# The experts' stage with TensorE in written order and the survey cut into parts

## The chip, the cores and the metric

The kernel runs on one core of a Trainium2 chip. Times are device microseconds (us) of one execution of the whole program. Five engines work side by side, each on its own queue of instructions: TensorE (PE, with its weight loads shown apart as PEld), VectorE (DVE), ScalarE (ACT), GpSimd (POOL) and SyncE (SP, which here only issues DMAs). An engine takes its instructions in order and each waits for what it needs from the others.

## The reference

Input x is 32 sequences of 256 tokens with 128 features, 8192 tokens in all, in f32. Two pre-norm layers follow each other. Each line below adds to x, and LN is a layer norm without weights.

```
x = x + causal_attention(LN(x))      # layer 0, 16 heads, queries and keys 128 wide per head
x = x + experts(LN(x))               # layer 0, 16 experts of width 64, and a shared one
x = x + hyperbolic_attention(LN(x))  # layer 1, 16 heads of 8
x = x + relu(LN(x) @ w1 + b1) @ w2 + b2
```

The experts are what this document is about:

```
scores = sigmoid(x @ gate_w.T);  choice = scores + e_bias
the best 2 of 4 groups of experts by the sum of their two best choices, then the best 4 experts in them
weight = scores of those 4 / their sum * 2.5
y = sum over the 4 of weight * (silu(x @ gate_e.T) * (x @ up_e.T)) @ down_e.T
y = y + (silu(x @ s_gate.T) * (x @ s_up.T)) @ s_down.T     # the shared expert
```

The kernel computes all 16 experts for every token and multiplies each hidden value by the token's weight for its expert, which is zero where the expert was not chosen.

## The kernel before

x stays in on-chip memory for the whole run, as 16 groups (`xg[g]`) of 512 tokens, four tiles of 128 tokens each. Four groups make a quad. The program goes through three stages.

1. `causal_attention`, up to about 1030 us. TensorE's order is written out by hand here (`tc.manual_schedule`), the other engines' order is the planner's.
2. `experts`, from about 1036 to 1520 us. This is the stage of the diff. It ends with a flag, read into a register, that picks the branch for layer 1.
3. `far_attention` with layer 1's feed-forward inside it, from about 1520 us. (The other branch, `hyperbolic_attention` and `feed_forward`, is in the program but not run on these inputs.) In it, `scores` (line 1118 on) makes two PSUM tiles, `sc0` and `sc1`, for the products of four heads.

The planner is the part of the compiler that orders instructions wherever no order is written by hand. It walks the program with estimated durations and, on each engine, takes what is ready, with what was written earlier first. So written order matters to it, but it also runs ahead. Which buffer an instruction may write is part of what it must wait for: a pool gives each tag a number of buffers, and a tile waits until its buffer's last readers are done.

**The experts' stage.** For each group g, `fetched(g)` brings the normed and transposed tokens `bxT` (line 671) and the weights `wb`, broadcast over partitions, in two DMAs of 1 MB (line 677), from DRAM, on SP's queue. It is called one group ahead, at chunk 1. Then come nine chunks: eight of two experts each (128 hidden rows) and the shared expert (64 hidden rows). A chunk is:

- `g_ps` (line 696) and `u_ps` (line 698) on PE, each one f32 product of 128x128 by 128x512, which the trace shows as two matmul passes
- Silu of `g_ps` into `act` on ACT (line 700)
- `act` times `u_ps` on DVE (line 701), then times `wb` on DVE (line 703; not for the shared expert)
- the down product of `act` into `y_ps` on PE (line 704), which adds up over the nine chunks

[...] After the nine chunks ACT copies the sum into `yT` (line 708), `add_transposed` turns it back with four PE transposes (line 109, in the PSUM tag `u`) and DVE adds it to `xg[g]` (line 110).

**The survey** of the group follows (`survey`, lines 605 to 642). It prepares layer 1 and collects the extremes that decide the branch: statistics on DVE (lines 612, 613), subtraction of the mean on POOL (line 614), four PE transposes into `xc_ps` (line 620, tag `w`), the copy `sxc` on ACT (line 622), its store to DRAM on SP (line 623), then for two halves the products for queries and keys (line 628, tag `w`, eight passes in all), their squares on ACT (line 633) and sums on DVE (line 634), and last five operations on DVE (lines 637 to 642).

**The preparation** of the last quad's routing runs inside the same loop, as 26 `pieces`: statistics of four groups, their deviations, for each group `normed` (POOL, line 504), `tokens` (PE transposes `rxT_ps`, line 511) and `scored` (`logits`, line 520), then `best_groups`, and for each group `weights` (DVE, five operations of 128x1024 and some small ones) and `turned` (PE transposes `wT_ps`, line 579). One piece is called after chunks 1, 3, 5 and 7, so four per group, until they are used up in group 6.

PE's order in this stage is the planner's. In the lines that are written, each chunk's down product follows its own `g_ps` and `u_ps`, and a group's transposes and survey come between its last chunk and the next group's first one.

Of the kernel before, what the change touches and what calls it, by code (L numbers as in the profile page):

```python
# [9 lines left out]
F32 = mybir.dt.float32  # L10
BF16 = mybir.dt.bfloat16
AF = mybir.ActivationFunctionType
ALU = mybir.AluOpType
AX = mybir.AxisListType
PSUM = bass.MemoryType.PSUM

P = 128
B, N, D = 32, 256, 128
T = B * N
TG = 4  # L20
GT = TG * P
NG = T // GT
QUAD = 4
EPS = 1e-5

H = 16
DH = D // H
# [4 lines left out]
NE, INTER = 16, 64  # L32
# [8 lines left out]
class Net:  # L41
# [562 lines left out]

    def survey(self, pool, psum, g):

        nc = self.nc
        mv = pool.tile([P, TG, 2], F32, tag="smv", name=f"smv{g}")
        xn = pool.tile([P, TG, D], F32, tag="sxn", bufs=1, name=f"sxn{g}")
        for t in range(TG):  # L610
            st = pool.tile([P, nc.vector.BN_STATS_DIM], F32, tag="sst", bufs=4, name=f"sst{g}_{t}")
            nc.vector.bn_stats(st, self.xg[g][:, t, :])
            nc.vector.bn_aggr(mv[:, t, :], st)  # L613
            nc.gpsimd.tensor_scalar(xn[:, t, :], self.xg[g][:, t, :], mv[:, t, 0:1], None, ALU.subtract)  # L614
        rv = self.rv[:, g]
        nc.vector.tensor_scalar(rv, mv[:, :, 1], EPS, None, ALU.add)
        nc.vector.reciprocal(rv, rv)
        ps = psum.tile([P, GT], F32, tag="w", name=f"xc_ps{g}")
        for t in range(TG):
            nc.tensor.transpose(ps[:, t * P : (t + 1) * P], xn[:, t, :], self.ident)  # L620
        xc = pool.tile([P, GT], F32, tag="sxc", name=f"sxc{g}")
        nc.scalar.copy(xc, ps)
        nc.sync.dma_start(out=self.xc[g], in_=xc)
        n2 = pool.tile([P, TG, 2 * H], F32, tag="sn2", name=f"sn2_{g}")
        for i in range(2):
            qk = psum.tile([P, 2, 2 * D], F32, tag="w", name=f"sqk{g}_{i}")
            for t in range(2):
                nc.tensor.matmul(
                    qk[:, t], xc[:, (2 * i + t) * P : (2 * i + t + 1) * P], self.w_qkv[:, 0 : 2 * D],
                    start=True, stop=True,  # L630
                )
            sq = pool.tile([P, 2, 2 * D], F32, tag="ssq", bufs=1, name=f"ssq{g}_{i}")
            nc.scalar.activation(sq, qk, AF.Square)
            nc.vector.tensor_reduce(
                n2[:, 2 * i : 2 * i + 2], sq.rearrange("p t (h d) -> p t h d", d=DH), AX.X, ALU.add
            )
        nc.vector.tensor_mul(n2, n2, rv.unsqueeze(2).to_broadcast([P, TG, 2 * H]))
        nc.vector.tensor_reduce(self.ends[:, 0, g : g + 1], n2, AX.XY, ALU.min)
        nc.vector.tensor_reduce(self.ends[:, 1, g : g + 1], n2, AX.XY, ALU.max)
        ra = self.ra[:, g].rearrange("p t s h -> p t (s h)")  # L640
        nc.vector.tensor_scalar(ra, n2, -1.0, 1.0, ALU.mult, ALU.add)
        nc.vector.reciprocal(ra, ra)

    def survey_result(self, pool, psum):

# [12 lines left out]
    def experts(self, prep):  # L658
        nc, tc = self.nc, self.tc
        NCH = NE * INTER // P  # L660
        w_g, w_u, w_d, s_g, s_u, s_d = (self.w_e[n] for n in ("w_g", "w_u", "w_d", "s_g", "s_u", "s_d"))
        with (
            tc.tile_pool(name="mo", bufs=2) as pool,
            tc.tile_pool(name="mops", bufs=2, space=PSUM) as psum,
        ):

            def fetched(g):


                xT = pool.tile([P, GT], F32, tag="xT", bufs=3, name=f"bxT{g}")  # L670
                nc.sync.dma_start(out=xT, in_=self.xt[g])
                wb = pool.tile([P, NCH, GT], F32, tag="wb", bufs=3, name=f"wb{g}")
                rows = self.rows[g].rearrange("(c e) t -> e c t", e=2)
                for c in range(0, NCH, 1 if g == 0 else NCH):
                    cs = slice(c, c + 1 if g == 0 else NCH)
                    for e in range(2):
                        nc.sync.dma_start(
                            out=wb[e * INTER : (e + 1) * INTER, cs], in_=rows[e, cs].partition_broadcast(INTER)
                        )
                return xT, wb  # L680

            pieces = self.preparation(NG // QUAD - 1, prep, psum, "w")
            ready = fetched(0)
            for g in range(NG):
                xT, wb = ready
                y_ps = psum.tile([P, GT], F32, tag="y", name=f"y_ps{g}")
                for c in range(NCH + 1):
                    if c == 1 and g + 1 < NG:
                        ready = fetched(g + 1)
                    shared = c == NCH  # L690
                    m = INTER if shared else P
                    wg = s_g if shared else w_g[:, c * P : (c + 1) * P]
                    wu = s_u if shared else w_u[:, c * P : (c + 1) * P]
                    wd = s_d if shared else w_d[:, c, :]
                    g_ps = psum.tile([P, GT], F32, tag="g", name=f"g_ps{g}_{c}")
                    nc.tensor.matmul(g_ps[:m, :], wg, xT, start=True, stop=True)  # L696
                    u_ps = psum.tile([P, GT], F32, tag="u", name=f"u_ps{g}_{c}")
                    nc.tensor.matmul(u_ps[:m, :], wu, xT, start=True, stop=True)  # L698
                    act = pool.tile([P, GT], F32, tag="act", bufs=3, name=f"act{g}_{c}")
                    nc.scalar.activation(act[:m, :], g_ps[:m, :], AF.Silu)  # L700
                    nc.vector.tensor_mul(act[:m, :], u_ps[:m, :], act[:m, :])  # L701
                    if not shared:
                        nc.vector.tensor_mul(act, act, wb[:, c])  # L703
                    nc.tensor.matmul(y_ps, wd, act[:m, :], start=c == 0, stop=shared)  # L704
                    if c % 2 == 1 and pieces:
                        pieces.pop(0)()
                yT = pool.tile([P, GT], F32, tag="yT", name=f"yT{g}")
                nc.scalar.copy(yT, y_ps)
                self.add_transposed(pool, psum, "u", g, yT)
                self.survey(pool, psum, g)  # L710
            self.survey_result(pool, psum)


# [793 lines left out]
```

## Time and profile before

| | us |
|---|---|
| median of the 3 runs | 2210.81 (2207.41 to 2212.19) |
| profiled execution, its own time | 2204.17 |
| span in the profile, first to last instruction | 2202.4 |
| experts' stage, first `g_ps` to the flag's last reduction | 1036.2 to 1518.1 |
| copies of `yT`, first and last of 16 | 1063.1 and 1503.5 |

Rows of the profile begin with the start and the length in us on the timeline, then engine, line, operation, the tiles written and read, their shapes and how many instructions were merged. What stands in square brackets is how long the engine had been idle before, and whose work ended that. In the list of waits the numbers are the total in us, the number of times and the longest. "PEclk" or "clock" is the share of its full clock that PE was granted. PE's busy time counts a matmul from its start to a modelled end, and successive matmuls overlap.

### The profile page before, as it was taken

Reading aid. Unit: us, or ns where it says so; the run is one execution under the profiler, and the core shown is the slowest. Engines: PE = TensorE matmul, PEld = TensorE weight load, DVE = VectorE, ACT = ScalarE, POOL = GpSimd, SP = SyncE. Lnnn points to the kernel's source line nnn. Section 1 sums busy time; section 2 is a strip of 40 time slices with the busy share of each in tenths; the row PEclk is TensorE's granted clock in tenths of the full one; section 3 lists DMA queues with packets and bytes.
Section 4 is the critical chain, followed back from the end, with each engine's and each line's share of the span. In section 5 each row is a group of like instructions: output and inputs, shape, how many; then the busy total and the mean of one; then the engine's idle time right before and its main releaser. Section 6 shows DMA issues by size and latency. Waiting matters only on the chain.

```text
span 2202.4 us, 38323 instructions
## 1 busy us (share of the span) xinstructions
PE 2063.9 (94%) x14083; PEld 1326.1 (60%) x14083; DVE 1517.5 (69%) x4804; ACT 1376.4 (62%) x2429; POOL 753.8 (34%) x841
## 2 busy tenths in 40 slices
PE   5999999999999999997999999996889999999997
PEld 4677777776777777774444433343556565665653
DVE  2666666569655875577558755554678888888885
ACT  1766677666776667663222222222888999999993
POOL 3000000100011000100111100001999999999994
PEclk8999999999999999998999999997899999999999
DMA  5000000000000000001743444400000000000000
GB/s 155 1 1 1 1 1 1 11 11 3 2 6 11 7 2 1 11 11 48 165 96 83 97 96 96 96 10 25 10 6 11 16 11 20 11 15 16 11 11 21
DMA packets 43940, 66.64 MB, mean 30 GB/s; under 512 B 3617, under 2 KB 16689, under 8 KB 43745
## 3 DMA queue, kind: packets, MB, share of 16 engines
q1 hardware_dynamic: 40960, 59.00, 11.2%
q0 software_dynamic: 1200, 3.78, 0.5%
q8 instruction: 114, 1.87, 0.3%
q10 hardware_dynamic: 1584, 1.34, 0.2%
q14 instruction: 82, 0.66, 0.1%
HBM read 50.99 MB, written 13.11 MB: 29 GB/s over the span
## 4 chain that ended last, share of the span: by engine, by line
PE 66%; DVE 14%; ACT 6%; POOL 6%; issue 6%; DMA 1%; POOLq 0%; ACTq 0%; SPq 0%; DVEq 0%
PE t_ps L258 10%; PE s L286 9%; PE y_ps L704 5%; PE fs L1123 5%; PE s L279 4%; PE g_ps L696 4%; DVE fv L1183 4%; PE av L335 4%; PE u_ps L698 3%; PE fav L1135 3%; POOL fv L1193 3%; PE pa_ps L316 3%; ACT ft L1177 2%; PE pb_ps L322 2%; PE pa_ps L315 2%
## 5 line engine op out<-in xcount | busy, mean ns | idle before, releaser
L1193 POOL TENSOR_TENSOR fv<-ft,fv 128x512 f32<-128x512 f32 x512 | 587.8, 1196 | 20.9 <-ACT fv L1188 20.9
L273 DVE CUSTOM_DVE_ANT_0 p<-s,mask 128x128 f32<-128x128 f32 (+1 forms) x1024 | 316.0, 353 | 296.4 <-PE s L279 176.0
L301 ACT ACTIVATE p<-p,lo 128x128 f32<-128x128 f32 (+1 forms) x1024 | 373.6, 444 | 162.8 <-DVE lo L295 162.7
L1183 DVE SCALAR_TENSOR_TENSOR fv<-fs,ft 128x1024 f32<-128x1024 f32 x256 | 300.5, 1216 | 23.3 <-ACT ft L1177 23.3
L1177 ACT ACTIVATE ft<-fs 128x1024 f32<-128x1024 f32 x256 | 247.9, 1020 | 49.1 <-PE fs L1123 40.1
L286 PE MATMUL s<-xT,tT 128*128 128x256 f32 x1024 | 265.6, 382 | 9.0 <-DVE lo L273 9.0
L258 PE MATMUL t_ps<-xT,m_all 128*128 128x512 f32 x512 | 252.9, 614 | 3.2 <-ACT score L525 1.9
L1188 ACT ACTIVATE fv<-fv 128x2048 f32<-128x2048 f32 x128 | 246.6, 1927 | 0.0
L700 ACT ACTIVATE act<-g_ps 128x512 f32<-128x512 f32 x144 | 85.9, 596 | 233.3 <-PE g_ps L696 219.1
L216 POOL TENSOR_TENSOR x<-x,w_bp 128x512 f32<-128x512 f32 x16 | 21.6, 1348 | 611.1 <-DVE xn L213 553.8
L1123 PE MATMUL fs<-fqT,fkT 32*128 32x256 f32 x2048 | 196.3, 408 | 28.2 <-DVE fv L1183 28.1
L286 PEld LDWEIGHTS s<-xT,tT 128*128 128x128 f32 x1024 | 177.4, 193 | 25.0 <-DVE lo L273 11.6
L1123 PEld LDWEIGHTS fs<-fqT,fkT 32*128 32x128 f32 x2048 | 124.2, 185 | 102.5 <-issue 43.6
L504 POOL TENSOR_SCALAR rxn<-x,rmv,rrstd 128x128 f32<-128x128 f32 x64 | 51.2, 811 | 375.7 <-PE rxT_ps L511 223.2
L614 POOL TENSOR_SCALAR sxn<-x,smv 128x128 f32<-128x128 f32 x64 | 44.8, 716 | 385.1 <-DVE smv L613 265.0
L259 ACT ACTIVATE tT<-t_ps,m_bias 128x512 f32<-128x512 f32 x256 | 161.0, 672 | 21.3 <-PE t_ps L258 20.9
L279 PEld LDWEIGHTS s<-xT,tT 128*128 128x128 f32 x1024 | 134.4, 192 | 60.2 <-issue 56.6
L701 DVE TENSOR_TENSOR act<-u_ps,act 128x512 f32<-128x512 f32 x144 | 97.7, 680 | 97.7 <-PE u_ps L698 89.4
L1135 PE MATMUL fav<-fv,fva 128*32 128x257 f32 x2048 | 142.0, 388 | 12.0 <-ACT fqT L1335 4.7
L696 PE MATMUL g_ps<-bxT,w_w_g 128*128 128x512 f32 x256 | 133.9, 609 | 3.1 <-DMA bxT<-xt 3.1
L258 PEld LDWEIGHTS t_ps<-xT,m_all 128*128 128x128 f32 x512 | 87.1, 192 | 81.2 <-issue 50.5
L704 PE MATMUL y_ps<-act,w_w_d 128*128 128x512 f32 x256 | 134.0, 616 | 1.4 <-DVE act L703 0.5
(222 smaller groups left out, 3678.2 us busy)
## 6 DMA issues: line engine op xcount, KB each, us to landing
wb<-rows SPq DMA_DIRECT2D x30, 1024.0 KB, 8.0
xt<-rxT SPq DMA_DIRECT2D x16, 256.0 KB, 2.0
bxT<-xt SPq DMA_DIRECT2D x16, 256.0 KB, 7.6
xc<-sxc SPq DMA_DIRECT2D x16, 256.0 KB, 2.1
fxc<-xc SPq DMA_DIRECT2D x16, 256.0 KB, 2.7
out<-x SPq DMA_DIRECT2D x16, 256.0 KB, 2.3
x<-in_x SPq DMA_DIRECT2D x8, 256.0 KB, 10.7
x<-in_x POOLq DMA_DIRECT2D x8, 256.0 KB, 10.3
```

The source lines that it names most:

```text
L258: nc.tensor.matmul(ps, m_all[:, h], G["xT"], start=True, stop=True)
L273: nc.vector.tensor_tensor_reduce(out=out, in0=x, in1=m, scale=-scale, scalar=3e38, op0=ALU.add, op1=ALU.min, accum_out=accum)
L279: nc.tensor.matmul(s0[:, j], tT[:, j, o : o + P], xT[:, o : o + P], start=True, stop=True)
L286: nc.tensor.matmul(s[:, l], tT[:, j + l, o + P : o + N], xT[:, o : o + N], start=True, stop=True)
L301: nc.scalar.activation(p[:, l], p[:, l], AF.Exp, bias=lo[:, c, l : l + 1], scale=-1.0)
L696: nc.tensor.matmul(g_ps[:m, :], wg, xT, start=True, stop=True)
L704: nc.tensor.matmul(y_ps, wd, act[:m, :], start=c == 0, stop=shared)
L1123: nc.tensor.matmul(sc[j // 2][:, j % 2, kc], kT[rows, kc * P : (kc + 1) * P], qT[rows], start=True, stop=True)
L1177: nc.scalar.activation(t[i], sc[i], AF.Relu, scale=-4.0)
L1183: nc.vector.scalar_tensor_tensor(v[:, 2 * i : 2 * i + 2, :, 0:N], sc[i], 0.5, t[i], ALU.subtract, ALU.mult)
L1188: nc.scalar.activation(v[:, :, :, 0:N], v[:, :, :, 0:N], AF.Sqrt, scale=-4.0)
L1193: nc.gpsimd.tensor_sub(v[:, j, :, 0:N], t[j // 2][:, j % 2], v[:, j, :, 0:N])
```

## The change

The loop over groups is now written for PE in order (`manual_schedule` for PE; the other engines stay with the planner). Three things move:

- A chunk is split into `hidden` (its `g_ps` and `u_ps`, Silu and the two DVE products) and `add` (the down product, and for the shared expert the copy of `yT`). `add` is called two chunks later than its `hidden`, across the border of groups too. The tag `act` has four buffers in place of three.
- `survey` no longer does its work at once but returns five parts: `centred`, `turned`, two `product`s and `ends`. `finish` puts `add_transposed` (now in the PSUM tag `w`) in front of the first. The parts of group g are called after chunks 2, 4, 5, 6 and 7 of group g+1, those of the last group behind the loop.
- The preparation's pieces are called after chunks 1, 3 and 8, three per group.

The operations and their number are the same. The diff, cut to its core (the bodies of the survey's parts are the old lines, moved into the inner functions):

```diff
     def survey(self, pool, psum, g):
...
+        made = {}
+
+        def centred():
...
+        def turned():
+            ps = psum.tile([P, GT], F32, tag="w", name=f"xc_ps{g}")
+            for t in range(TG):
+                nc.tensor.transpose(ps[:, t * P : (t + 1) * P], made["xn"][:, t, :], self.ident)
+            xc = made["xc"] = pool.tile([P, GT], F32, tag="sxc", name=f"sxc{g}")
+            nc.scalar.copy(xc, ps)
+            nc.sync.dma_start(out=self.xc[g], in_=xc)
+
+        def product(i):
...
+        def ends():
...
+        return [centred, turned, lambda: product(0), lambda: product(1), ends]
...
+            def hidden(g, c, xT, wb):
...
+                g_ps = psum.tile([P, GT], F32, tag="g", name=f"g_ps{g}_{c}")
+                nc.tensor.matmul(g_ps[:m, :], wg, xT, start=True, stop=True)
+                u_ps = psum.tile([P, GT], F32, tag="u", name=f"u_ps{g}_{c}")
+                nc.tensor.matmul(u_ps[:m, :], wu, xT, start=True, stop=True)
+                act = pool.tile([P, GT], F32, tag="act", bufs=4, name=f"act{g}_{c}")
+                nc.scalar.activation(act[:m, :], g_ps[:m, :], AF.Silu)
+                nc.vector.tensor_mul(act[:m, :], u_ps[:m, :], act[:m, :])
+                if not shared:
+                    nc.vector.tensor_mul(act, act, wb[:, c])
+
+                def add():
+                    if c == 0:
+                        sums[g] = psum.tile([P, GT], F32, tag="y", name=f"y_ps{g}")
+                    nc.tensor.matmul(sums[g], wd, act[:m, :], start=c == 0, stop=shared)
+                    if shared:
+                        yT = sums[g, "T"] = pool.tile([P, GT], F32, tag="yT", name=f"yT{g}")
+                        nc.scalar.copy(yT, sums[g])
+
+                return add
+
+            def finish(g):
+
+                first, *others = self.survey(pool, psum, g)
+
+                def added():
+                    self.add_transposed(pool, psum, "w", g, sums[g, "T"])
+                    first()
+
+                return [added, *others]
+
+            sums, waiting, rest = {}, [], []
             pieces = self.preparation(NG // QUAD - 1, prep, psum, "w")
             ready = fetched(0)
-            for g in range(NG):
-                xT, wb = ready
...
-                    nc.tensor.matmul(y_ps, wd, act[:m, :], start=c == 0, stop=shared)
-                    if c % 2 == 1 and pieces:
-                        pieces.pop(0)()
-                yT = pool.tile([P, GT], F32, tag="yT", name=f"yT{g}")
-                nc.scalar.copy(yT, y_ps)
-                self.add_transposed(pool, psum, "u", g, yT)
-                self.survey(pool, psum, g)
+            with tc.manual_schedule(engines={mybir.EngineType.PE}):
+                for g in range(NG):
+                    xT, wb = ready
+                    for c in range(NCH + 1):
+                        if c == 1 and g + 1 < NG:
+                            ready = fetched(g + 1)
+                        waiting.append(hidden(g, c, xT, wb))
+                        if len(waiting) > 2:
+                            waiting.pop(0)()
+
+                        if c == 2 and g:
+                            rest = finish(g - 1)
+                        if c in (2, 4, 5, 6, 7) and rest:
+                            rest.pop(0)()
+                        elif c in (1, 3, 8) and pieces:
+                            pieces.pop(0)()
+                for f in waiting + finish(NG - 1):
+                    f()
             self.survey_result(pool, psum)
```

The change in a few words also names the far path's two tiles for four heads' products. No line of `far_attention` differs between the two files.

More of the change, by code (lines that the diff above doesn't have):

```diff
@@ L607, in survey @@
         nc = self.nc
[L608 to L614, printed above, removed]
-        rv = self.rv[:, g]
[L616 to L625, printed above, removed]
+        rv = self.rv[:, g]
+        made = {}
+        def centred():
+            mv = pool.tile([P, TG, 2], F32, tag="smv", name=f"smv{g}")
+            xn = made["xn"] = pool.tile([P, TG, D], F32, tag="sxn", bufs=1, name=f"sxn{g}")
+            for t in range(TG):
+                st = pool.tile([P, nc.vector.BN_STATS_DIM], F32, tag="sst", bufs=4, name=f"sst{g}_{t}")
+                nc.vector.bn_stats(st, self.xg[g][:, t, :])
+                nc.vector.bn_aggr(mv[:, t, :], st)
+                nc.gpsimd.tensor_scalar(xn[:, t, :], self.xg[g][:, t, :], mv[:, t, 0:1], None, ALU.subtract)
+            nc.vector.tensor_scalar(rv, mv[:, :, 1], EPS, None, ALU.add)
+            nc.vector.reciprocal(rv, rv)
+        def turned():
+            ps = psum.tile([P, GT], F32, tag="w", name=f"xc_ps{g}")
+            for t in range(TG):
+                nc.tensor.transpose(ps[:, t * P : (t + 1) * P], made["xn"][:, t, :], self.ident)
[3 more added lines that the diff above has]
+        def product(i):
+            if i == 0:
+                made["n2"] = pool.tile([P, TG, 2 * H], F32, tag="sn2", name=f"sn2_{g}")
             qk = psum.tile([P, 2, 2 * D], F32, tag="w", name=f"sqk{g}_{i}")
@@ L628, in survey @@
                 nc.tensor.matmul(
-                    qk[:, t], xc[:, (2 * i + t) * P : (2 * i + t + 1) * P], self.w_qkv[:, 0 : 2 * D],
+                    qk[:, t], made["xc"][:, (2 * i + t) * P : (2 * i + t + 1) * P], self.w_qkv[:, 0 : 2 * D],
                     start=True, stop=True,
@@ L634, in survey @@
             nc.vector.tensor_reduce(
-                n2[:, 2 * i : 2 * i + 2], sq.rearrange("p t (h d) -> p t h d", d=DH), AX.X, ALU.add
+                made["n2"][:, 2 * i : 2 * i + 2], sq.rearrange("p t (h d) -> p t h d", d=DH), AX.X, ALU.add
             )
[L637 to L642, printed above, removed]
+        def ends():
+            n2 = made["n2"]
+            nc.vector.tensor_mul(n2, n2, rv.unsqueeze(2).to_broadcast([P, TG, 2 * H]))
+            nc.vector.tensor_reduce(self.ends[:, 0, g : g + 1], n2, AX.XY, ALU.min)
+            nc.vector.tensor_reduce(self.ends[:, 1, g : g + 1], n2, AX.XY, ALU.max)
+            ra = self.ra[:, g].rearrange("p t s h -> p t (s h)")
+            nc.vector.tensor_scalar(ra, n2, -1.0, 1.0, ALU.mult, ALU.add)
+            nc.vector.reciprocal(ra, ra)
+        return [centred, turned, lambda: product(0), lambda: product(1), ends]
     def survey_result(self, pool, psum):
@@ L680, in fetched @@
                 return xT, wb
+            def hidden(g, c, xT, wb):
+                shared = c == NCH
+                m = INTER if shared else P
+                wg = s_g if shared else w_g[:, c * P : (c + 1) * P]
+                wu = s_u if shared else w_u[:, c * P : (c + 1) * P]
+                wd = s_d if shared else w_d[:, c, :]
+                g_ps = psum.tile([P, GT], F32, tag="g", name=f"g_ps{g}_{c}")
[15 more added lines that the diff above has]
+                return add
@@ L682, in experts @@
+            def finish(g):
[5 more added lines that the diff above has]
+            sums, waiting, rest = {}, [], []
             pieces = self.preparation(NG // QUAD - 1, prep, psum, "w")
             ready = fetched(0)
-            for g in range(NG):
-                xT, wb = ready
[L686 to L704, printed above, removed]
-                    if c % 2 == 1 and pieces:
-                        pieces.pop(0)()
-                yT = pool.tile([P, GT], F32, tag="yT", name=f"yT{g}")
-                nc.scalar.copy(yT, y_ps)
-                self.add_transposed(pool, psum, "u", g, yT)
-                self.survey(pool, psum, g)
```

## The prediction

> **What bounds the kernel now.** I read the page first (busy shares, slices), then the stretches by time, then the waits of the experts' stage, then its timeline for one group.
>
> ```profile
> PE 2063.9 (94%) x14083; PEld 1326.1 (60%) x14083; DVE 1517.5 (69%) x4804; ACT 1376.4 (62%) x2429; POOL 753.8 (34%) x841
> PE t_ps L258 10%; PE s L286 9%; PE y_ps L704 5%; PE fs L1123 5%; PE s L279 4%; PE g_ps L696 4%; DVE fv L1183 4%; PE av L335 4%; PE u_ps L698 3%; PE fav L1135 3%; POOL fv L1193 3%; PE pa_ps L316 3%; ACT ft L1177 2%; PE pb_ps L322 2%; PE pa_ps L315 2%
> ```
>
> The matmul engine is the bound, by busy share and in the chain that ended last. The diff touches only the experts' stage, about 1036 to 1520 us. Its stretches, cut at the copies of yT that end each group (columns: length, then busy us and count of PE, PEld, DVE, ACT, POOL, then clock, DMA share, GB/s):
>
> ```profile
> 1154.40:1186.60 32.20, 31.16 (x85) 13.59 (x86) 26.91 (x60) 9.16 (x17) 2.81 (x4) 1.00 0.41 94
> 1186.60:1217.70 31.10, 28.94 (x79) 12.14 (x79) 28.81 (x58) 8.55 (x15) 3.35 (x4) 1.00 0.40 87
> 1273.20:1302.00 28.80, 27.79 (x71) 11.47 (x72) 16.55 (x35) 7.74 (x14) 2.70 (x4) 1.00 0.42 92
> 1503.50:1520.00 16.50, 6.71 (x18) 3.73 (x17) 6.29 (x25) 2.67 (x5) 2.68 (x5) 0.57 0.04 16
> ```
>
> Groups 7 to 15 take 28.80 us each, all alike; groups 1 to 6, which also carry the last quad's preparation, take 181.3 us together (1063.1 to 1244.4). Every group runs at clock 1.00, so there is no throttle to win or lose. DVE is at 16.6 of 28.8 us except in groups 4 and 5, where the ranking fills it.
>
> **A rule against the busy row.** By that row PE idles 28.80 - 27.79 = 1.0 us per group, so at most 15 x 1.0 = 15 us could be won. [...]
>
> ```profile
> 1361.69 1.02 PE L696 MATMUL g_ps<-bxT,w_w_g 128*128 128x512 f32 x2
> 1362.51 2.70 POOL L614 TENSOR_SCALAR sxn<-x,smv 128x128 f32<-128x128 f32 x4 [26.09 <-DVE smv L613]
> 1363.16 0.33 PE L620 MATMUL xc_ps<-ident,sxn 128*128 128x128 f32 x1 [0.45 <-POOL sxn L614]
> 1364.68 0.33 PE L620 MATMUL xc_ps<-ident,sxn 128*128 128x128 f32 x1 [0.22 <-POOL sxn L614]
> 1365.26 0.33 PE L620 MATMUL xc_ps<-ident,sxn 128*128 128x128 f32 x1 [0.25 <-POOL sxn L614]
> 1372.39 1.02 PE L696 MATMUL g_ps<-bxT,w_w_g 128*128 128x512 f32 x2
> 1372.76 0.69 DVE L703 TENSOR_TENSOR act<-act,wb 128x512 f32<-128x512 f32 x1
> 1373.51 1.13 PE L704 MATMUL y_ps<-act,w_w_d 128*128 128x512 f32 x2
> 1381.60 0.69 DVE L703 TENSOR_TENSOR act<-act,wb 128x512 f32<-128x512 f32 x1
> 1382.45 1.02 PE L704 MATMUL y_ps<-act,w_w_d 128*128 128x512 f32 x2
> 1386.12 1.13 PE L704 MATMUL y_ps<-act,w_w_d 128*128 128x512 f32 x2
> ```
>
> A 128x512 f32 product is two passes of 0.429 us, start to start, when nothing is late; a survey pass (L628) 0.215, a transpose 0.108. Beyond that, the group from 1359.43 to 1388.23 loses 3.07 us:
> - 1.66 us around the survey: the pass at 1362.12 is followed 1.04 us later, and two transposes 0.39 and 0.47 us late, for POOL's subtractions; 0.08 us before L628.
> - 0.62 us where a y_ps product waits for DVE's product just finished (1372.76 + 0.69 = 1373.45, y at 1373.51): 0.26 and two of 0.03 late, and 0.10 more each time in the first pass. At 1382.45 act had been ready since 1382.29 and nothing was lost: a wait already met is free.
> - 0.73 us where the shared expert's 64-wide weights come and go (1386.12 is one of four places).
> - 0.06 us of roundings.
>
> By cadence the removable part is 3.07 - 0.73 = 2.34 us, over twice the busy row's. I take the cadence: starts are measured, ends of matmuls modelled.
>
> **The change, part by part.**
>
> *The far path's two tiles.* The diff has nothing on it; `scores` in far_attention already makes two tiles sc0 and sc1. Cost 0.
>
> *Down products two chunks late, PE as written.* A chunk is g, u and the y of two chunks ago: 3 x 0.858 = 2.57 us. L701 starts 1.13 us after its u (1383.31 to 1384.44) and the pair L701, L703 takes 1.41 us, so act is ready 0.86 + 1.13 + 1.41 = 3.40 us after its chunk's start. y comes at 2 x 2.57 + 1.72 = 6.86 us: 3.46 us of cover. Saves the 0.62 us. The fourth act buffer serves this; no PE instruction is added.
>
> *The survey as parts in the next group's chunks 2, 4, 5, 6, 7.* The yT transposes come at chunk 2, behind g, u, y: about 3.4 us after the shared y starts, where 1387.18 to 1388.97 shows 1.79 needed. From their start to POOL's fourth subtraction took 1360.40 to 1365.21, 4.81 us; the centred transposes now follow at 0.43 + 2 x 2.57 = 5.57 us: 0.76 us of cover. Then L628 follows one chunk (2.57 us) after them, where 1.03 us are needed (1365.26 to 1366.29). Saves the 1.66 us.
>
> *What queues behind.* PE can no longer go round a late operand: a transpose waiting for POOL holds every g and u behind it, and ACT and DVE behind those. The smallest cover is POOL's 0.76 us; each delay of the add L110 beyond it costs one for one. [...] The nearest row is the attention stage, already written for PE this way: from 100 to 900 us PE waited 8.4 us in all. I go with the row.
>
> *DVE, ACT, POOL, SP.* Their work is the same; their order is still the planner's. DVE can park on L634, waiting for a square, in front of act products. In the present groups:
>
> ```profile
> DVE sn L634 <- ACT ssq L633: 26.3, 18, 2.2
> PE xc_ps L620 <- POOL sxn L614: 8.3, 27, 0.4
> ```
>
> That is 2.9 us of parking per group (1244 to 1503). Under 3.46 us of cover it should mostly vanish; bounds 0 and 1.5 us per group; I take 0.3, close to the covered end, because DVE has 10 us free: 15 x 0.3 = 4.5 us. ACT is at 7.7 us. The two table loads (1.28 us each, at 1035 and 1038) remain, hidden or not as now. POOL's four subtractions per normed piece (3.1 us) sit at chunk 8 mostly, away from the survey's.
>
> SP: the store of sxc (0.33 us to issue) moves behind the next group's fetch of bxT and wb (three issues); its reader is the far path at 1521.7, and the last one goes out as now. wb lands in 8.0 us against some 23 us of lead. Without the lead PE would wait those 8 us.
>
> *Preparation pieces: three per group, not four.* 26 pieces end in group 8 instead of 6. Group 12's fetch is called in group 11, at least two groups later, so hidden. PE's part stays 4 x (0.43 + 0.9 + 0.43) = 7.0 us. DVE's excess over 16.5 us in groups 4 to 6 (10.4 + 12.3 + 3.4 = 26 us) must fit into some 86 us with 31 free, but turned pieces now hold PE in order: each weights piece is about 7 us of DVE, and one turned follows by two chunks. Bounds 0 (DVE runs ahead, as it ran the statistics of group 1's pieces before 1036) and 13 us; I take 4.
>
> *Start and tail.* The first six products and the 16.5 us behind the last yT keep their order: 0.
>
> **The sum.** Groups 7 to 15: 9 x 2.34 = 21.1. Groups 1 to 6 lose 20.0 us by the same count, less 6 x 0.73: 15.6. Together 36.7. Less 4.5 and 4: 28.2 us. The profiled execution takes 2204.2 us (span 2202.4), so 2176.0. The median shown is 2210.8, 6.6 higher; the same 28.2 off gives **2182.6 us**, 1.3% faster, and groups 9 to 15 at about 26.75 us.
>
> **Rivals.**
> - *Half is eaten.* DVE's or POOL's order delays PE by 1.2 us per group: 36.7 - 4 - 18 = 14.7, so 2196. For: L634's parking and POOL's cover of 0.76. Against: 10 us of free DVE time.
> - *No difference.* The stage finds another limit at its present pace, say the act chain or wb, or the written order comes out like the planner's: 2211. Against: DMA share 0.42, DVE 16.6 of 28.8.
> - *Slower.* DVE parks on L634 for each of the two products in front of an act product: by the times above, u two chunks on stalls up to 1.8 us per product, 3.6, plus 0.4 at L110: 4.0 us per group against 2.34 won. 15 x 1.66 = 25, so 2236. It decides from 2.34 us of stall per group. For: the wait row. Against: the planner would have to queue it that way in nearly all groups.
>
> **How the numbers follow.** Forecast 0.62, half 0.22, no difference 0.05, slower 0.11. A measurement tells about 0.2% (4.4 us) from nothing. So faster 0.84, same 0.05, slower 0.11. The forecast's own range is 2171 (all 36.7 won, with the runs' spread) to 2192; the half reaches to 2204. The range 2171 to 2204 leaves out slower, same and about 0.03 below. Forecast and half are both gains, so one range serves.
>
> **What would show it.** Right: yT copies 26.5 to 27 us apart in late groups; the row of PE waiting for POOL sxn gone or under 2 us; y_ps 0.86 us after u throughout; the stages before 1036 and after the flag unchanged. Wrong: PE waits at the survey's transposes or at u for DVE; groups 6 to 8 over 32 us; a slower far path.

## The result and the profile after

The changed kernel takes 2175.03 us (median of 4 runs, 2170.94 to 2177.22), the kernel before 2211.44 in the same measurement. The ratio is 0.9837, with a 95% interval of 0.9816 to 0.9858: 36.4 us faster, where 28.2 were forecast.

The stretches of the changed kernel, cut at its copies of yT (columns as before: length, then busy us and count of PE, PEld, DVE, ACT, POOL, then clock, DMA share, GB/s):

```profile
1090.70:1118.50 27.80, 27.80 (x83) 13.31 (x83) 16.66 (x36) 8.54 (x16) 6.34 (x8) 1.00 0.51 114
1201.90:1229.70 27.80, 27.32 (x75) 12.24 (x76) 26.53 (x54) 8.27 (x14) 3.28 (x4) 1.00 0.42 91
1311.00:1337.50 26.50, 26.50 (x71) 12.01 (x72) 16.65 (x36) 7.72 (x14) 2.70 (x4) 1.00 0.47 98
1466.60:1483.10 16.50, 6.61 (x17) 3.73 (x17) 6.38 (x25) 3.14 (x5) 2.85 (x5) 0.69 0.04 16
```

A late group takes 26.51 us where it took 28.80, and PE's busy time now equals the length. The operations of DVE and ACT are the same as before. With DVE at 26.5 of 27.8 us (second row, the ranking) the group is no longer than its neighbours that carry other pieces. The tail, from the last yT to the flag, keeps its length: 14.6 us before, 14.4 after.

PE's own waits within the stage (columns: total us, times, longest), from 1063 to 1503 us in the kernel before,

```profile
PE xc_ps L620 <- POOL sxn L614: 14.5, 42, 1.2
```

and from 1063 to 1466 us in the changed one:

```profile
PE xc_ps L626 <- POOL sxn L619: 0.7, 3, 0.2
```

One group of the changed kernel on the timeline, with the columns of the prediction's timeline:

```profile
1342.23 2.70 POOL L619 TENSOR_SCALAR sxn<-x,smv 128x128 f32<-128x128 f32 x4 [23.81 <-DVE smv L618]
1344.75 1.02 PE L715 MATMUL y_ps<-act,w_w_d 128*128 128x512 f32 x2
1345.61 0.60 PE L626 MATMUL xc_ps<-ident,sxn 128*128 128x128 f32 x4
1346.05 1.02 PE L703 MATMUL g_ps<-bxT,w_w_g 128*128 128x512 f32 x2
1355.60 1.07 PE L703 MATMUL g_ps<-bxT,w_s_g 128*64 128x512 f32 x2
1357.46 1.12 PE L715 MATMUL y_ps<-act,w_w_d 128*128 128x512 f32 x2
```

POOL's fourth subtraction ends at 1344.93, the transposes start at 1345.61, 0.86 us behind the product in front of them: nothing is lost, and the cover is 0.68 us. Start to start, the group from 1337.34 loses 0.77 us, and 0.74 of it are the four places where the 64-wide weights come and go (the last two rows are two of these).

The whole programs are compared best by the stage alone, from its first g_ps to its last yT copy, because it begins anywhere from 1033.4 to 1043.3 us in these profiles, although the order of instructions in the attention in front is the same:

| kernel | stage, us | late group, us | whole program, median us |
|---|---|---|---|
| before | 467.3 | 28.80 | 2211.4 |
| changed | 432.5 | 26.51 | 2175.0 |
| lag of one chunk | 437.6 | 26.51 | 2183.7 |
| no lag | 704.3 | 42.14 | 2449.6 (one run) |
| PE left to the planner | 432.4 | 26.51 | 2171.1 |
| transposes a chunk early | 465.2 | 28.19 | 2208.1 |
| lag alone, planner | 458.0 | 28.28 | 2198.6 |
| parts alone, planner | 440.0 | 27.06 | 2176.2 |
| three act buffers | 432.5 | 26.51 | 2175.4 |
| parts at once, PE as written | 541.4 | about 34.0 | 2282.7 |
| four pieces per group | 443.1 | 26.51 | 2182.4 |
| shared expert padded | 422.0 | 25.78 | 2163.9 |

The stage gained 34.8 us. The profiled spans differ by 34.7 (2202.4 and 2167.7): the stage began 2.2 us sooner and what follows the last yT took 2.2 us longer. The cause of that stays open; it takes from 698.9 to 704.0 us over all these profiles.

Counted start to start over the whole stage, with 0.429 us for a pass of 512 columns, 0.215 for 256 and 0.108 for a transpose, PE's instructions need 416 us in both kernels. Before the change PE lost 51.7 us beyond that, after it 16.9. The difference is the 34.8 us. Of what is left, 11.3 us are the changes of the weights' shape, 2.8 the half clock in which the stage begins (0.50 from 1034.0 to 1039.3 us), 1.25 waits for POOL in groups 6 and 7, and 0.8 the wait for the last copy of yT, behind which no chunk follows.

### The profile page after: what moved, and what is told of

It is laid out like the page before. It is cut to its first block, busy times and chain, and to the rows that moved or that the text cites. A ratio compares the mean times of both kernels' runs of the same rounds, so it can differ in the third digit from the quotient of the medians.

```text
span 2167.7 us, 38331 instructions
## 1 busy us (share of the span) xinstructions
PE 2044.2 (94%) x14083; PEld 1333.0 (61%) x14083; DVE 1518.2 (70%) x4804; ACT 1377.1 (64%) x2429; POOL 753.8 (35%) x841
## 4 chain that ended last, share of the span: by engine, by line
PE 70%; DVE 15%; ACT 6%; issue 4%; POOL 3%; DMA 1%; POOLq 0%; ACTq 0%; SPq 0%; DVEq 0%
PE t_ps L258 10%; PE s L286 9%; DVE fv L1225 6%; PE g_ps L703 6%; PE y_ps L715 5%; PE u_ps L705 5%; PE s L279 5%; PE fs L1165 4%; PE av L335 4%; PE pa_ps L316 3%; ACT ft L1219 3%; PE fav L1177 3%; PE pb_ps L322 2%; PE pa_ps L315 2%; POOL fv L1235 2%
## 5 line engine op out<-in xcount | busy, mean ns | idle before, releaser
L279 PE MATMUL s<-xT,tT 128*128 128x128 f32 x1024 | 134.9, 275 | 0.0
## 6 DMA issues: line engine op xcount, KB each, us to landing
x<-in_x POOLq DMA_DIRECT2D x8, 256.0 KB, 10.2
```

Source lines behind the costliest of these rows:

```text
L279: nc.tensor.matmul(s0[:, j], tT[:, j, o : o + P], xT[:, o : o + P], start=True, stop=True)
```

## The experiments

The theory going in was cover: PE runs without a gap when every operand is ready before PE reaches it, so the gain is the sum of two removed waits, and a place in the order is good or bad by its cover in microseconds. The rivals were that the order written for PE brings the gain by itself, or that one of the two waits carries nearly all of it.

### How much cover is needed

One chunk of lag:

```diff
-                        if len(waiting) > 2:
+                        if len(waiting) > 1:
```

> The down product comes one chunk late instead of two. Theory (cover): act is ready 3.40 us after its chunk's start, 3.55 at worst in the changed kernel's late groups, and y now comes at 2.57 + 1.72 = 4.29 us, so 0.7 us of cover are left and nothing is lost in late groups (yT copies 26.5 us apart); a few us at most where the ranking fills DVE: 2175 to 2182. Rival (two chunks are needed, DVE's order jitters by more than a chunk): at least 0.5 us per group, 2183 and more.

It took 2183.67 us (2176.87 to 2186.56; ratio to the kernel before 0.9876, 0.9854 to 0.9897), 1.7 us above the theory's range and inside the rival's. But the rival's half a microsecond in every group is not there: late groups are 26.513 us apart, as with two chunks. So one chunk is enough cover there. The stage takes 5.1 us more: about 3 in groups 5 to 7, where the ranking delays DVE (one late transpose alone waited 1.9 us), and about 2 at the start. There the first down product waits 1.45 us for act, behind the load of the Silu table (1.28 us) and a PE at half its clock (pairs of passes start 1.70 us apart, in place of 0.86). The second chunk of lag pays for such places only. The rest of the difference lies outside the stage, mostly in front of it: it began at 1043.3 us in this profile.

No lag:

```diff
-                        if len(waiting) > 2:
+                        if len(waiting) > 0:
```

> The down product comes right behind its own chunk's u, with PE in written order and the survey's parts as in the changed kernel. Theory (cover): y is reached 1.72 us after its chunk's start and act is ready at 3.45, so each of eight chunks stalls 1.73 us and 0.1 more for the late weight load, the shared one 1.1: 15.7 us per group, 16 groups, 252 us: about 2427. Rival (the lag is worth only the 0.62 us per group that the kernel before lost at y): 2175 + 10 = 2185.

One run took 2449.55 us, and late groups are 42.14 us apart: 15.63 us over 26.51, where 15.7 were expected. The 22 us above the expected total come from six groups: four that carry pieces (45.2 to 51.0 us) and two late ones (43.6 and 44.1). In each of the six the granted clock stood at half for 3.4 to 10.2 us; over the whole run its mean was 0.976, in the changed kernel 0.981.

The centred transposes one chunk sooner:

```diff
-                        if c in (2, 4, 5, 6, 7) and rest:
+                        if c in (2, 3, 5, 6, 7) and rest:
                             rest.pop(0)()
-                        elif c in (1, 3, 8) and pieces:
+                        elif c in (1, 4, 8) and pieces:
```

> The centred transposes come after chunk 3 instead of 4 (a piece of the preparation takes chunk 4). Theory (cover): in the changed kernel POOL's fourth subtraction ends 0.68 us before the transposes start, so one chunk (2.57 us) earlier they stall 1.9 us and up to 0.1 more for a late load, in 15 groups: 2175 + 30 = 2205, late groups 28.5 us apart. Rival (PE has slack elsewhere, or the subtractions move with the transposes): 2175.

It took 2208.14 us (ratio to before 0.9994, 0.9984 to 1.0004): one step in the order gives back nearly the whole gain (the stage takes 465.2 us, before the change 467.3). PE's waits from 1030 to 1480 us in this kernel:

```profile
PE xc_ps L626 <- POOL sxn L619: 19.4, 44, 1.4
```

Late groups are 28.19 us apart, 1.68 over 26.51, near the missing cover (2.57 - 0.68 = 1.89). Two groups where the ranking also delayed DVE's statistics, and where the clock then fell to half for 3.4 us (its mean was 0.54 from 1258.9 to 1262.5 us), took 32.6 and 33.9 us.

### Which edit does it

PE's order left to the planner:

```diff
-            with tc.manual_schedule(engines={mybir.EngineType.PE}):
+            if True:
                 for g in range(NG):
```

> The changed kernel with PE's order left to the planner again; the lag, the parts and their places in the text stay. Theory (the written order is what keeps the survey's transposes behind POOL): the planner puts the transposes two products behind those of yT again, where POOL needs 4.8 us, so the 1.66 us per group come back: 2175 + 25 = 2200, with PE waiting for POOL sxn some 0.9 us per group. Rival (cutting and placing the parts does it, whoever orders PE): 2175.

It took 2171.08 us (2170.43 to 2175.41; ratio 0.9836, 0.9819 to 0.9853). The theory's 2200 is wrong here and the rival right. Compared instruction by instruction, this program and the changed one have the same order on all five engines. This fits a planner that takes what is ready with the earliest written first: with the new places in the text every operand would be ready by its estimate when its turn comes, so it has nothing to reorder. (Its estimates themselves were not seen.) The `manual_schedule` of the change does nothing here.

The lag alone, under the planner, with the survey whole:

```diff
-            with tc.manual_schedule(engines={mybir.EngineType.PE}):
+            if True:
...
-                        if c in (2, 4, 5, 6, 7) and rest:
-                            rest.pop(0)()
+                        if c == 2 and rest:
+                            while rest:
+                                rest.pop(0)()
```

> PE's order is the planner's, the down product is written two chunks late, and the survey is not cut: all its parts are written after chunk 2 of the next group. Theory (the place in the text decides, the planner only fills in): y's 0.62 us per group stay won, but the transposes come as early as the planner's short estimate of POOL lets them, so 1.66 us per group come back, 15 groups: 2171 + 25 = 2196. Rival (the lag is most of the gain, the survey's cut little): under 2180.

It took 2198.58 us (ratio 0.9951, 0.9937 to 0.9966). PE's waits from 1300 to 1480 us:

```profile
PE xc_ps L626 <- POOL sxn L619: 7.5, 21, 0.9
```

That is the wait of the kernel before, again in about its old size: late groups lose 28.28 - 26.51 = 1.77 us, where 1.66 were read before the change.

The parts alone, under the planner, with no lag:

```diff
-                        if len(waiting) > 2:
+                        if len(waiting) > 0:
...
-            with tc.manual_schedule(engines={mybir.EngineType.PE}):
+            if True:
```

> PE's order is the planner's, the survey's parts stand where the changed kernel has them, and each down product is written right behind its own chunk. Theory (the place in the text decides): the survey's 1.66 us per group stay won; y is placed as soon as the planner holds act to be ready, which is just late, so the 0.62 us per group come back: 2171 + 10 = 2181. Rival (without the lag the planner keeps y in text order and PE stalls as with written order and no lag): far over 2209.

It took 2176.18 us (ratio 0.9861, 0.9828 to 0.9893), a little under the expected 2181. Late groups lose 27.06 - 26.51 = 0.55 us. PE's weight loads waited from 1280 to 1460 us:

```profile
PEld y_ps L715 <- DVE act L710: 25.9, 47, 1.1
```

The same row in the kernel before, from 1244 to 1503 us:

```profile
PEld y_ps L704 <- DVE act L703: 35.2, 54, 0.9
```

The changed kernel has no such row from 1280 to 1440. Most of this waiting, some 3.9 us per group (25.9 us in 180), is hidden behind the matmul in front; what shows in the length of a group is the 0.55 us.

A late group gains 28.80 - 28.28 = 0.52 us by the lag alone and 1.74 by the parts alone, together 2.26, and 2.29 with both edits: the two waits are nearly independent, and the survey's is about three quarters of the gain. Over the stage the two gain 467.3 - 458.0 = 9.3 and 27.3 us, together 36.6, where both edits gain 34.8. These two sums also hold what both programs keep of the change: three pieces per group, and the survey beginning behind the next group's third chunk. In group 5 of the kernel before, where the ranking fills DVE, PE lost 1.5 us to late act products (start to start). Neither program has that loss, so it is counted twice. The three pieces in the old order were not run alone.

The same text as the lag alone, with PE in written order:

```diff
-                        if c in (2, 4, 5, 6, 7) and rest:
-                            rest.pop(0)()
+                        if c == 2 and rest:
+                            while rest:
+                                rest.pop(0)()
```

> As the run with the lag alone (all the survey's parts written after chunk 2), but PE in written order. Theory (cover): PE stands at the centred transposes until POOL is done, 4.81 - 0.43 = 4.4 us, and at L628 for the copy, 0.7 us and some for late loads: 5.3 us per group, 15 groups, 80 us: about 2252. Rival (the written order itself brings the gain): under 2180.

Two runs took 2282.58 and 2282.86 us (ratio 1.0347, 1.031 to 1.038), slower than before the change by 3.5%. One text gives 458 us of stage under the planner and 541 in written order. The loss was 31 us larger than expected, 7.1 to 7.6 us per late group in place of 5.3. Stretches and timeline of one group show why:

```profile
1350.20:1353.10 2.90, 1.76 (x4) 0.69 (x4) 0.23 (x2) 0.59 (x1) 1.71 (x3) 0.55 0.00 0
1353.10:1357.40 4.30, 4.28 (x9) 3.21 (x10) 0.69 (x1) 1.06 (x2) 0.00 (x0) 0.51 0.20 65
1357.40:1378.60 21.20, 21.20 (x49) 8.57 (x48) 12.35 (x21) 5.16 (x10) 0.00 (x0) 1.00 0.30 65
```

```profile
1350.22 0.33 PE L626 MATMUL xc_ps<-ident,sxn 128*128 128x128 f32 x1 [2.27 <-POOL sxn L619]
1350.81 1.64 PE L626 MATMUL xc_ps<-ident,sxn 128*128 128x128 f32 x3 [0.25 <-POOL sxn L619]
1353.12 3.78 PE L636 MATMUL sqk<-w_w_qkv,sxc 128*128 128x256 f32 x8 [0.68 <-ACT sxc L628]
```

The stall costs twice. From 1347.8 to 1353.1 PE does four transposes only, 4.9 us are lost in waiting, and from 1350.5 on the granted clock is at half (0.50 until 1357.3). The eight passes of L636 start 0.427 us apart in place of 0.215, which is 1.7 us more, and the g_ps behind them is late too, and takes 1.18 us to the next product in place of 0.86.

### The smaller edits

Three act buffers:

```diff
-                act = pool.tile([P, GT], F32, tag="act", bufs=4, name=f"act{g}_{c}")
+                act = pool.tile([P, GT], F32, tag="act", bufs=3, name=f"act{g}_{c}")
```

> Three act buffers instead of four, all else as changed. Theory: Silu of chunk c needs the buffer of chunk c-3, whose down product PE has run before it starts chunk c, so nothing waits: 2171 to 2176, within 4 us. Rival (the fourth buffer carries part of the gain): ACT waits for y_ps in each chunk and DVE's act products come later, 0.5 us per group or more: 2180 and more.

It took 2175.42 us, its stage the same 432.5 us. The fourth buffer serves nothing.

Four pieces per group:

```diff
-                        elif c in (1, 3, 8) and pieces:
+                        elif c in (0, 1, 3, 8) and pieces:
```

> A piece of the preparation after chunks 0, 1, 3 and 8, four per group as before the change. Theory (DVE's time is the limit where the ranking runs): the 26 us of ranking fall into groups 4 to 6 again, where DVE needs more than 26.5 us per group, so PE waits for wt or act some 3 to 8 us once: 2175 to 2182. Rival (three per group changes nothing): 2171 to 2174.

It took 2182.42 us (ratio 0.989, 0.9863 to 0.9917), at the theory's end. PE's waits from 1065 to 1480 us, and two stretches:

```profile
PE wT_ps L579 <- DVE wt L574: 8.1, 1, 8.1
```

```profile
1179.50:1189.00 9.50, 1.35 (x6) 0.52 (x5) 9.50 (x14) 0.59 (x1) 0.00 (x0) 0.69 0.63 127
1189.00:1193.00 4.00, 4.00 (x7) 1.74 (x6) 4.00 (x7) 1.17 (x2) 0.00 (x0) 0.50 0.04 8
```

One transpose of the ranking's weights waits 8.1 us for DVE, which is busy for the whole 9.5 us; then PE runs at half clock for 4 us more. So three pieces per group are worth 10.6 us of stage in this order.

### What was left

The shared expert's weights filled up with zeros to 128x128 (and `m = P` in `hidden`):

```diff
-        self.w_e = {n: self.load(keep, n, eng) for n in ("w_g", "w_u", "w_d", "s_g", "s_u", "s_d")}
+        self.w_e = {n: self.load(keep, n, eng) for n in ("w_g", "w_u", "w_d")}
+        for n in ("s_g", "s_u", "s_d"):
+            src = self.w[n]
+            t = self.w_e[n] = keep.tile([P, P], F32, name=f"w_{n}")
+            self.nc.gpsimd.memset(t, 0.0)
+            eng.dma_start(out=t[0 : src.shape[0], 0 : src.shape[1]], in_=src)
```

> The shared expert's three weights stand in 128x128 tiles filled up with zeros, so its products are 128 wide like the others (the added hidden rows are zero); all else as changed. Theory (the 0.73 us per group left over come from the change of the weights' shape): they vanish, 16 x 0.73 = 12 us: 2160 to 2163, late groups 25.8 us apart. Rival (they come from waits or from the shared chunk's place): 2171 to 2176, no change.

It took 2163.93 us (2159.82 to 2168.16; ratio to before 0.9801, 0.9767 to 0.9834), 0.9 us above the theory's range. In the same measurement the kernel with three act buffers, whose stage is the changed kernel's, took 2175.42. The stage is 10.5 us shorter than the changed kernel's, not 12: the changes of shape gave 11.3, and the waits for POOL in groups 6 and 7 grew from 1.25 to 2.0. A late group:

```profile
1301.30:1327.10 25.80, 25.80 (x71) 12.56 (x70) 16.58 (x36) 7.74 (x13) 2.70 (x4) 1.00 0.47 101
```

26.51 - 25.78 = 0.73 us per group is what the count from start to start had put down to the shape of the weights, and by the same count a late group now loses 0.03. More work in the array is faster here. Of the kernels run, this is the fastest.

## Why the prediction was right, and where it was off

*The cadence, not the busy row.* Right: 2.29 us per late group were won where the cadence promised 2.34 and the busy row 1.0. The 2.34 hold 0.06 us of roundings, which are no wait: 1.66 + 0.62 = 2.28. The 0.73 us set aside for the change of shape stayed, and went when the shape was made equal.

*Each wait's size.* Right: 1.66 and 0.62 us were read from one group's timeline; removing one alone leaves 1.77 and 0.55 us.

*The covers.* Right: 0.76 us for POOL's fourth subtraction (measured 0.68), and 3.46 us for y, of which one chunk can be taken away in late groups and two can't. The fourth act buffer, which the prediction says serves this, is not needed for it: with three the order on every engine and the stage are the same.

*The two reserves.* Too large, and they are the term of the sum that was mis-sized. DVE's parking, "I take 0.3" per group, 4.5 us in all, cost nothing that can be seen: a late group loses 0.77 us, and all but 0.03 of it is the change of shape. DVE still waits at the squares, 14.2 us in 16 times from 1244 to 1466 where it was 26.3 in 18, but under the cover of y. The ranking, "I take 4", measured 1.25 us, the waits for POOL in groups 6 and 7, where it stands among the statistics on DVE. With some 0.9 us of roundings counted as removable in 15 groups, this is about what lies between the 36.7 us and the stage's 34.8; the forecast was 28.2. The size of the ranking hangs on where its pieces stand: with four per group the stage takes 10.6 us more.

*PE as written.* The prediction followed the change in listing "PE as written" with the lag, and weighed the risk that "PE can no longer go round a late operand". On this text there is nothing to go round, and the planner makes the same order. As a risk the step was right, and under-priced: at once and in written order it cost 7.1 to 7.6 us per late group, since the clock falls as well (to 0.50). "No throttle to win or lose" holds for the change as it stands, not for this risk.

*The rivals.* Half eaten, no difference and slower did not come. The slower rival's mechanism, DVE parked on L634, was not seen to hold up PE in late groups; the two runs that did go slower were slowed by act coming late for y (no lag) and by POOL's subtractions (parts at once), with the clock in both (mean 0.976 and 0.964, in the changed kernel 0.981).

## What to carry to other kernels

Where recorded matmuls overlap, as here (0.593 us long, 0.429 us from start to start), read PE's headroom from start to start and list every excess of one period by its cause: here the three causes found that way were later each removed alone, within 0.1 us of the size read. Then give each operand its cover in microseconds by where its reader stands in the text; a reader one chunk too early cost nearly as much as the whole change won. In this stage it was the place in the text that did it: written by hand or left to the planner the order was the same, and where an operand was late the hand-written order cost 83 us of stage more.

## What the hardware showed that was not expected

The clock fell to half in the middle of a busy stage. With the survey's parts at once in written order PE did four transposes only from 1347.8 to 1353.1 us and was at no time without a matmul for more than 2.3 us; this is the clock (columns as in the stretches above):

```profile
1347.10:1350.50 3.40, 1.13 (x6) 0.50 (x4) 3.23 (x13) 0.00 (x0) 0.93 (x2) 1.00 0.80 149
1350.50:1357.30 6.80, 5.66 (x13) 3.75 (x13) 0.69 (x1) 1.55 (x3) 1.41 (x3) 0.50 0.12 41
```

Stalls of 1.7 us once per group (the transposes a chunk early) left the clock at 1.00 in late groups (1320 to 1348 us). Without a lag PE stalls 1.7 us in each of eight chunks, and the clock fell in two of the late groups, for 3.4 us each. With the parts at once the stretch at half clock was 6.8 us long (second row). Before that fall PE was not idle throughout: it was busy for 1.13 of the 3.40 us (first row). How thin the work must be is not shown by these runs. So a stall's price can have a step in it: here 6.8 us at half clock came with 4.9 us of waiting. With the stalls of this stage before the change it did not come: from 1041.5 to 1505.7 us its clock was 1.00 throughout.

In late groups of these kernels a matmul with another shape of weights than the one before (64 wide against 128) cost 0.14 to 0.20 us at each change, although the weights had been in on-chip memory since about 54 us and PE's rows in the profile show no wait for another engine there. With equal shapes a late group loses 0.03 us in all. At four changes per group this was 2.8% of a late group.
